# Graph attention and graph convolution in fp32: scores in seven half-size products over node halves of two graphs

## The chip, the cores and the metric

The kernel runs on one core of one Trainium2 chip. A core has TensorE (matrix multiplication, called PE in the profile), VectorE (DVE), ScalarE (ACT), GpSimd (POOL) and SyncE (SP, which here only issues transfers). Each engine works through its own instructions in order and waits for the others by semaphores. The metric is the time of one execution in microseconds of device time, and the figure compared is the median of several runs.

## What is computed

The input is 64 graphs of 256 nodes with 512 features each, and one 256 x 256 adjacency matrix per graph, all in fp32. Two layers follow each other, each with a residual:

```python
h = jnp.maximum(_layernorm(x, axis=-1), 0.0)
# layer 0: attention along the adjacency
query = jnp.einsum('bnd,od->bno', h, Wq_w) + Wq_b
keyt = jnp.einsum('bnd,od->bno', h, Wk_w) + Wk_b
value = jnp.einsum('bnd,od->bno', h, Wv_w) + Wv_b
weight = jnp.einsum('bqd,bkd->bqk', query, keyt)
weight = adj * jnp.exp(weight)
weight = weight / jnp.sum(weight, axis=2, keepdims=True)
x = x + jnp.einsum('bqk,bkd->bqd', weight, value)
# layer 1: graph convolution
h = jnp.maximum(_layernorm(x, axis=-1), 0.0)
A_hat = adj + jnp.eye(adj.shape[-1])
d_inv_sqrt = A_hat.sum(axis=-1) ** (-0.5)
L = A_hat * d_inv_sqrt[:, :, None] * d_inv_sqrt[:, None, :]
x = x + jnp.einsum('bij,bjf->bif', L, h @ W + b)
```

## The kernel before

The graphs are handled in 32 pairs (G = 2 graphs at a time, p is the number of the pair). A pair has 512 rows of x, held as four tiles of 128 rows (TB = 4), so that all projections work on 512 nodes at once. Query and key weights are multiplied into one matrix beforehand, so that the scores are h times a projected "key side" g.

Three of the large products of a pair are 512 x 512 x 512 each: the key side g (`key_side`), the values v (`values`) and the product of the aggregated features with the second layer's weight (`convolve`). Each is computed in `seven_products` (L321): a 2 x 2 block product with seven half-size products in place of eight, at the price of sums of blocks before and after. The sums of the features are t1 to t4 in the tile hS, made in `feature_sums` (L308) on GpSimd for every pair but the first. The feature matrix is stored transposed as hT, features over partitions and nodes along the free side. In it b11 and b21 are the columns of the first graph, b12 and b22 those of the second, with the first index for the half of the features. The sums of the weights are made once. The seven results land in three PSUM banks; a bank that holds one product is read by VectorE or ACT (first, u2, u3, c22) before a second product is added in the same bank, so that those two products depend on a quick reader.

The scores are not done in this way. `attend` (L464) handles one graph after the other. For each of two blocks of 128 keys it accumulates four matmuls with g as the stationary side and the graph's 256 query columns of hT as the moving one (L472). ACT takes the exponential out of PSUM into wT (L482), VectorE multiplies by the transposed adjacency aT (L483, both operands in SBUF), and then wT is the stationary side of the output matmuls (L493) against v. A column of ones in v gives the row sums. VectorE divides and adds into x (L503). After it GpSimd adds the identity to the diagonal blocks of aT (L741) and the value bias to x of the next pair (L683), and VectorE measures the rows for the second norm (L244).

`convolve` (L545) first aggregates: h times aT, four groups (`aggregate`, L551), each with two feature blocks and two blocks of nodes, and 256 columns moving (L555). The results and their sums are in yS, and the seven products with the second weight follow (pm_w). Their results are scaled by the degree and added into x by VectorE (`scaled`, L590) and GpSimd (`into`, L597). At the end of `second_layer` GpSimd makes the feature sums of the pair after next, and VectorE transposes its adjacency out of the tile aq, whose 32 x 32 blocks were placed by the transfers (`transposed_adjacency`, L452).

One step of the main loop for pair p is: `first_layer(p)` (attention), `project(p + 1)` (key side and values of the next pair, with norms and block transposes of pair p + 2 between), loads of x and adjacency for p + 3, and `second_layer(p)`. The order in which the instructions stand on each engine is set by a scheduler from these calls; `tc.issue_after` puts work behind a named instruction. The pools say how many buffers there are: xp has four for x, ap three for the adjacency, p1 one for each tag, p2 two, and PSUM eight banks. A load into a buffer waits for the last use of what was in it, and for x this is the transfer to the output. All these transfers are issued by SP, in one queue.

Of the kernel before, what the change touches and what calls it, by code (L numbers as in the profile page):

```python
# [16 lines left out]
def kernel(  # L17
# [29 lines left out]

    nc = tc.nc
# [16 lines left out]
    xp = ctx.enter_context(tc.tile_pool(name="xp", bufs=4))  # L65
    ap = ctx.enter_context(tc.tile_pool(name="ap", bufs=3))
# [7 lines left out]

    def load_x(p):
        x_tiles[p] = xp.tile([P, TB, D], F32, tag="x", name=f"x_{p}")
        nc.sync.dma_start(
            x_tiles[p], x[G * p : G * p + G].rearrange("g (nb p) d -> p (g nb) d", p=P)
        )

    def load_a(p):
        a_tiles[p] = ap.tile([P, TB, N], F32, tag="a", name=f"a_{p}")
        nc.sync.dma_start(
            a_tiles[p], adj[G * p : G * p + G].rearrange("g (nb p) k -> p (g nb) k", p=P)
        )
# [105 lines left out]
    def bias_products():  # L191
# [4 lines left out]
        g_rows, last = weighted_rows(wq_rows, bkT, "A2")  # L196
# [111 lines left out]
    def feature_sums(p, hT):  # L308
# [3 lines left out]
        hS = p1.tile([P, 4, 2, N], F32, tag="hS", name=f"hS_{p}")  # L312
        t1, t2, t3, t4 = (hS[:, i] for i in range(4))
# [3 lines left out]
        eng.tensor_tensor(t3, b22, b12, sub)  # L317
        eng.tensor_tensor(t4, b21, t2, sub)
        return (b11, b21, b22, t1, t2, t3, t4)
# [125 lines left out]
    def transposed_adjacency(p):  # L445
        a = a_tiles[p]
        aT = p2.tile([P, TB, N], F32, tag="aT", name=f"aT_{p}")
        if p > 0:
            out_view = aT.rearrange("p (g kt) q -> p kt g q", g=G)
            in_view = q_tiles[p].rearrange("p kt (g j) r -> p kt g (j r)", g=G)  # L450
            for kt in range(NB):
                nc.vector.transpose(out_view[:, kt], in_view[:, kt])  # L452
            return aT
        for g in range(G):
            pt = ps_m.tile([P, NB, N], F32, tag="pm", name=f"pt_a_{p}_{g}")
            for kb in range(NB):
                for qb in range(NB):
                    nc.tensor.transpose(  # L458
                        pt[:, kb, ts(qb, P)], a[:, g * NB + qb, ts(kb, P)], ident
                    )  # L460
            nc.scalar.copy(aT[:, g * NB : (g + 1) * NB, :], pt)
        return aT

    def attend(p, hT, gT, ks, aT):  # L464

        xt = x_tiles[p]
        wT = p1.tile([P, TB, N], F32, tag="wT", name=f"wT_{p}")
        for g in range(G):
            pm = ps_m.tile([P, NB, N], F32, tag="pm", name=f"pm_s_{p}_{g}")
            for kb in range(NB):  # L470
                for oc in range(DC):
                    nc.tensor.matmul(  # L472
                        pm[:, kb, :],
                        gT[:, oc, ts(g * NB + kb, P)],
                        hT[:, oc, ts(g, N)],
                        start=oc == 0,
                        stop=oc == DC - 1,
                    )
            rows = slice(g * NB, (g + 1) * NB)
            for kb in range(NB):  # L480
                t = g * NB + kb
                nc.scalar.activation(wT[:, t, :], pm[:, kb, :], AF.Exp, bias=ks[:, t : t + 1])  # L482
            nc.vector.tensor_tensor(wT[:, rows, :], wT[:, rows, :], aT[:, rows, :], mult)  # L483
        for g in range(G):
            for qb in range(NB):
                t = g * NB + qb
                rsum = sm.tile([P, 1], F32, tag="rsum", name=f"rsum_{p}_{t}")
                for half in range(2):
# [3 lines left out]
                    for kb in range(NB):  # L492
                        nc.tensor.matmul(  # L493
                            pm[:, 0:width],
                            wT[:, g * NB + kb, ts(qb, P)],
                            v[:, g * NB + kb, lo : lo + width],
# [6 lines left out]
                    last = nc.vector.scalar_tensor_tensor(xh, pm[:, 0:HD], rsum, xh, mult, add)  # L503
        return last.ins
# [13 lines left out]
    def weighted_degrees(p, d, row):  # L518
# [3 lines left out]
        scratch = p1.tile([P, D], F32, tag="scratch", name=f"ad_{p}")  # L522
        for t in range(TB):
            nc.vector.scalar_tensor_tensor(  # L524
                scratch[:, 0:N],
                a[:, t, :],
                1.0,
                row[:, ts(t // NB, N)],
# [16 lines left out]
    def convolve(p, h, aT, d, moved, then_t4, then_first):  # L545
# [5 lines left out]
        def aggregate(fh, g):  # L551
# [294 lines left out]
```

## Time and profile before

| what | value |
|---|---|
| median of 3 runs | 1861.83 us (1861.76 to 1861.85) |
| profiled execution | 1864.19 us, span of the profile 1862.4 us |
| PE busy | 1849.9 us (99%), 8578 matmul records and as many weight loads |
| DVE, ACT, POOL busy | 1235.8 us (66%), 760.8 us (41%), 641.8 us (34%) |
| matmuls by tile, records of 128x256 or 128x257 | pm_w 1792, pm_g 1792, pm_v 1792, pm_o 1024, pm_s 1024, pm_l 1024 |
| transfers | 114.83 MB, mean 62 GB/s; 1024 KB of x land 6.5 us after issue, the output 4.5 us |
| granted clock of TensorE | 0.998 |

One pair in mid-run takes 57.00 us. Its stages, by the engines' busy time in stretches of the profile (us from the start of the span; in each column the busy time and, in brackets, the number of instructions):

```profile
core 0: us, PE busy (x) PEld busy (x) DVE busy (x) ACT busy (x) POOL busy (x), PEclk, DMA share, GB/s
969.62:976.53 6.91, 6.91 (x34) 6.08 (x32) 2.78 (x5) 0.84 (x2) 4.79 (x6) 1.00 0.73 196
976.53:983.45 6.92, 6.92 (x33) 6.05 (x32) 5.71 (x16) 0.84 (x2) 5.08 (x6) 1.00 0.66 187
983.45:1007.63 24.18, 24.18 (x114) 21.27 (x113) 17.25 (x40) 13.17 (x21) 5.37 (x12) 1.00 0.03 8
1007.63:1014.53 6.90, 6.90 (x33) 6.08 (x32) 4.94 (x8) 1.17 (x2) 0.00 (x0) 1.00 0.04 14
1014.53:1026.62 12.09, 12.09 (x57) 10.64 (x56) 7.42 (x22) 7.80 (x14) 4.79 (x4) 1.00 0.13 44
```

The stretches are the scores, the outputs of the attention, the key side with the values, the aggregates, and the seven products with the second weight. A busy share of 100% on PE says that matmul records follow each other without a gap; PEld is the loading of the stationary side, which runs beside the matmuls. In the timeline a row is one group of like instructions: its start, its length from the first start to the last end, engine, line, operation, tiles and number, and in brackets the idle time of that engine before it with what ended it.

### The profile page before, as it was taken

To read this page: it belongs to the slowest core of one execution; us is meant where nothing else is said; L and a number is where in the kernel's file an instruction comes from. 1 tells how busy PE (TensorE), PEld (TensorE's weight loads), DVE (VectorE), ACT (ScalarE), POOL (GpSimd) and SP (SyncE) were. 2 spreads that over 40 slices of the span, in tenths; PEclk is the share of its full clock that TensorE was granted. 3 is DMA by queue.
4 is the path that set the end of the run, shared out by engine and by line. 5 is a ranking of instruction groups with operands and counts; after the bars stand their busy time and mean duration, and the time that the engine had idled before them with its cause. 6 is when DMAs were issued, how large, how long until landed. Compare 5 with 4: busy or idle time off the path is not lost.

```text
span 1862.4 us, 23484 instructions
## 1 busy us (share of the span) xinstructions
PE 1849.9 (99%) x8578; PEld 1625.5 (87%) x8578; DVE 1235.8 (66%) x2874; ACT 760.8 (41%) x1316; POOL 641.8 (34%) x839
## 2 busy tenths in 40 slices
PE   8999999999999999999999999999999999999998
PEld 7888888888888888888888888888888888888887
DVE  6866676666766666666667666666666676666745
ACT  3434443344434344443444344444434443344412
POOL 2443223432234432244322343322443223433222
PEclk9999999999999999999999999999999999999999
DMA  7322122221122231222221222202222112221001
GB/s 209 63 74 74 34 52 68 68 74 49 42 63 68 74 74 28 54 72 69 74 51 41 63 68 74 73 22 60 74 68 74 48 44 63 69 74 40 7 23 46
DMA packets 205908, 114.83 MB, mean 62 GB/s; under 512 B 148192, under 2 KB 168672, under 8 KB 205792
## 3 DMA queue, kind: packets, MB, share of 16 engines
q1 hardware_dynamic: 204672, 112.28, 23.0%
q8 instruction: 67, 1.10, 0.3%
q10 hardware_dynamic: 1056, 1.05, 0.2%
q14 instruction: 49, 0.40, 0.2%
q0 software_dynamic: 64, 0.00, 0.1%
HBM read 79.70 MB, written 33.62 MB: 61 GB/s over the span
## 4 chain that ended last, share of the span: by engine, by line
PE 98%; DVE 1%; DMA 1%; issue 0%; DVEq 0%; ACTq 0%
PE pm_g L338 21%; PE pm_w L338 21%; PE pm_v L338 21%; PE pm_o L493 12%; PE pm_l L555 12%; PE pm_s L472 11%; PE pm_mT L170 1%; DMA wq_rows<-in_L_gnn_Wq_w_dram 1%; DVE hc L275 0%; DVE ad L524 0%; PE pt_h L295 0%; PE pt_wv L220 0%; DVE aT L452 0%; DVE gT L389 0%; PE pt_a L458 0%
## 5 line engine op out<-in xcount | busy, mean ns | idle before, releaser
L338 PE MATMUL pm_w<-w_set,yS 128*128 128x256 f32 x1792 | 392.0, 379 | 0.0
L338 PEld LDWEIGHTS pm_w<-w_set,yS 128*128 128x128 f32 x1792 | 340.5, 190 | 46.3
L305 ACT COPY hT<-hq 32x512 f32<-32x512 f32 x496 | 305.5, 616 | 32.0 <-DVE hq L286 26.2
L597 POOL TENSOR_TENSOR x<-x,A_w 128x512 f32<-128x512 f32 x32 | 40.6, 1268 | 746.4 <-ACT A_w L588 746.4
L338 PE MATMUL pm_g<-hS,m_set 128*128 128x256 f32 x1024 | 236.5, 379 | 0.0
L338 PE MATMUL pm_v<-v_set,hS 128*128 128x256 f32 x1024 | 231.7, 379 | 1.5 <-DVE U_v L428 1.5
L493 PE MATMUL pm_o<-v,wT 128*128 128x257 f32 (+1 forms) x1024 | 226.8, 379 | 0.2 <-DVE wT L483 0.2
L472 PE MATMUL pm_s<-hT,gT 128*128 128x256 f32 x1024 | 226.4, 379 | 0.0
L555 PE MATMUL pm_l<-aT,h_b 128*128 128x256 f32 x1024 | 226.2, 379 | 0.0
L338 PEld LDWEIGHTS pm_v<-v_set,hS 128*128 128x128 f32 x1024 | 194.5, 190 | 28.3 <-DVE U_v L428 1.9
L493 PEld LDWEIGHTS pm_o<-v,wT 128*128 128x128 f32 x1024 | 193.7, 189 | 28.3 <-issue 0.5
L338 PEld LDWEIGHTS pm_g<-hS,m_set 128*128 128x128 f32 x1024 | 194.1, 190 | 27.1 <-DVE U_g L378 0.3
L555 PEld LDWEIGHTS pm_l<-aT,h_b 128*128 128x128 f32 x1024 | 194.6, 190 | 26.5
L472 PEld LDWEIGHTS pm_s<-hT,gT 128*128 128x128 f32 x1024 | 194.6, 190 | 26.5
L338 PE MATMUL pm_v<-v_set,hT 128*128 128x256 f32 x768 | 186.3, 379 | 0.0
L590 DVE SCALAR_TENSOR_TENSOR x<-pm_w,irr_d,x 128x256 f32<-128x256 f32 x256 | 112.1, 480 | 108.1 <-PE pm_w L338 82.6
L338 PE MATMUL pm_g<-hT,m_set 128*128 128x256 f32 x768 | 181.5, 379 | 0.0
L482 ACT ACTIVATE wT<-pm_s,ks 128x256 f32<-128x256 f32 x128 | 53.8, 471 | 290.8 <-PE pm_s L472 290.8
L338 PEld LDWEIGHTS pm_g<-hT,m_set 128*128 128x128 f32 x768 | 145.8, 190 | 20.4 <-issue 0.5
L338 PEld LDWEIGHTS pm_v<-v_set,hT 128*128 128x128 f32 x768 | 145.9, 190 | 19.8
L683 POOL TENSOR_TENSOR x<-x,bv_all 128x512 f32<-128x512 f32 x128 | 159.0, 1276 | 0.0
L483 DVE TENSOR_TENSOR wT<-wT,aT 128x512 f32<-128x512 f32 x64 | 44.3, 692 | 152.5 <-ACT wT L482 152.5
(119 smaller groups left out, 2085.6 us busy)
## 6 DMA issues: line engine op xcount, KB each, us to landing
x<-in_x_dram SPq DMA_DIRECT2D x32, 1024.0 KB, 6.5
out_dram<-x SPq DMA_DIRECT2D x31, 1024.0 KB, 4.5
a<-in_adj_dram SPq DMA_DIRECT2D x32, 512.0 KB, 3.9
aq<-in_adj_dram SPq DMA_DIRECT2D x124, 128.0 KB, 4.0
drow<-dflat SPq DMA_DIRECT2D x32, 256.0 KB, 5.0
wq_rows<-in_L_gnn_Wq_w_dram ACTq DMA_DIRECT2D x2, 512.0 KB, 8.4
wk_rows<-in_L_gnn_Wk_w_dram SPq DMA_DIRECT2D x2, 512.0 KB, 7.7
wv_rows<-in_L_gnn_Wv_w_dram SPq DMA_DIRECT2D x1, 1024.0 KB, 15.9
```

The source lines that it names most:

```text
L170: nc.tensor.matmul(pm, wk_rows[:, oc, ts(dc, P)], wq_rows[:, oc, ts(half, HD)], start=oc == 0, stop=oc == DC - 1,)
L305: last = nc.scalar.copy(dst[j * Q : (j + 1) * Q, i], src[i * Q : (i + 1) * Q, j])
L338: nc.tensor.matmul(banks[bank][:, r, :], left[:, ts(r, P)], right, start=start and r == 0 and dt == 0, stop=r == 1 and dt == 1, skip_group ...
L472: nc.tensor.matmul(pm[:, kb, :], gT[:, oc, ts(g * NB + kb, P)], hT[:, oc, ts(g, N)], start=oc == 0, stop=oc == DC - 1,)
L482: nc.scalar.activation(wT[:, t, :], pm[:, kb, :], AF.Exp, bias=ks[:, t : t + 1])
L483: nc.vector.tensor_tensor(wT[:, rows, :], wT[:, rows, :], aT[:, rows, :], mult)
L493: nc.tensor.matmul(pm[:, 0:width], wT[:, g * NB + kb, ts(qb, P)], v[:, g * NB + kb, lo : lo + width], start=kb == 0, stop=kb == NB - 1,)
L555: nc.tensor.matmul(pm[:, fi, :], h[:, g * NB + jb, ts(2 * fh + fi, P)], aT[:, g * NB + jb, :], start=jb == 0, stop=jb == NB - 1,)
L590: last = nc.vector.scalar_tensor_tensor(dst[:, r, :], pm[:, r, :], dr_, plus[:, r, :], mult, add)
L597: last = nc.gpsimd.tensor_tensor(block(i, g), block(i, g), more, add).ins
L683: nc.gpsimd.tensor_tensor(xh, xh, bv_all, add)
```

## The change

The scores become one seven-product scheme over the pair. For this the node halves are no longer the graphs: each graph's 256 nodes are split in two blocks of 128, and "half 0" is the first block of both graphs, "half 1" the second block of both. The tile order of x, adjacency, v and aT goes from graph-major to block-major (`p (nb g) k`). With this the sums t1 to t4 of the features serve the key side, the values and the scores. The score product is then, for each graph, keys in two blocks by queries in two blocks over two halves of the features: seven products, each of four matmuls (two graphs, two feature blocks) with 128 moving columns. The sums of the key side, s1 to s4, are made on GpSimd after each key side (`key_sums`); one of the four is written in place over a block of g, and likewise one feature sum over a block of hT. hS has two buffers instead of one, since the sums of a pair are now read until its attention.

The aggregates of `convolve` take a half of the nodes, so two graphs' blocks of 128 query columns in place of one graph's 256: twice as many matmuls, each with half the columns. The pools of x and of the adjacency lose one buffer each, and the loads for p + 3 move behind `second_layer(p)`. Each load of x and adjacency and each output transfer becomes two, one for each graph. The transposition of the adjacency for the pair after next moves from the end of the second layer to behind its u3 result, in four pieces of 256 columns instead of two of 512. One temporary (A2) goes; the second scaled copy is made in place.

The core of the diff:

```diff
-    xp = ctx.enter_context(tc.tile_pool(name="xp", bufs=4))
-    ap = ctx.enter_context(tc.tile_pool(name="ap", bufs=3))
+    xp = ctx.enter_context(tc.tile_pool(name="xp", bufs=3))
+    ap = ctx.enter_context(tc.tile_pool(name="ap", bufs=2))
...
+    def of_graph(tile_, g):
+        return tile_.rearrange("p (nb g) k -> p g nb k", g=G)[:, g]
+
+    def in_dram(t, p, g):
+        return t[G * p + g].rearrange("(nb p) k -> p nb k", p=P)
+
     def load_x(p):
         x_tiles[p] = xp.tile([P, TB, D], F32, tag="x", name=f"x_{p}")
-        nc.sync.dma_start(
-            x_tiles[p], x[G * p : G * p + G].rearrange("g (nb p) d -> p (g nb) d", p=P)
-        )
+        for g in range(G):
+            nc.sync.dma_start(of_graph(x_tiles[p], g), in_dram(x, p, g))
 
     def load_a(p):
         a_tiles[p] = ap.tile([P, TB, N], F32, tag="a", name=f"a_{p}")
-        nc.sync.dma_start(
-            a_tiles[p], adj[G * p : G * p + G].rearrange("g (nb p) k -> p (g nb) k", p=P)
-        )
+        for g in range(G):
+            nc.sync.dma_start(of_graph(a_tiles[p], g), in_dram(adj, p, g))
...
-        hS = p1.tile([P, 4, 2, N], F32, tag="hS", name=f"hS_{p}")
-        t1, t2, t3, t4 = (hS[:, i] for i in range(4))
+        hS = p2.tile([P, 3, 2, N], F32, tag="hS", name=f"hS_{p}")
+        t1, t2, t4 = (hS[:, i] for i in range(3))
         eng = nc.vector if p == 0 else nc.gpsimd
         eng.tensor_tensor(t1, b12, b11, sub)
         eng.tensor_tensor(t2, b22, t1, sub)
-        eng.tensor_tensor(t3, b22, b12, sub)
+
+        eng.tensor_tensor(b12, b22, b12, sub)
         eng.tensor_tensor(t4, b21, t2, sub)
-        return (b11, b21, b22, t1, t2, t3, t4)
+        return (b11, b21, b22, t1, t2, b12, t4)
+
+    def key_sums(p, gT):
+
+        a11, a21 = gT[:, 0:2, 0:N], gT[:, 0:2, N:NT]
+        a12, a22 = gT[:, 2:4, 0:N], gT[:, 2:4, N:NT]
+        gS = p1.tile([P, 3, 2, N], F32, tag="gS", name=f"gS_{p}")
+        s1, s2, s4 = (gS[:, i] for i in range(3))
+        nc.gpsimd.tensor_tensor(s1, a21, a22, add)
+        nc.gpsimd.tensor_tensor(s2, s1, a11, sub)
+
+        nc.gpsimd.tensor_tensor(a21, a11, a21, sub)
+        nc.gpsimd.tensor_tensor(s4, a12, s2, sub)
+        return (a11, a12, a22, s1, s2, a21, s4)
...
-        aT = p2.tile([P, TB, N], F32, tag="aT", name=f"aT_{p}")
+
+        aT = p2.tile([P, NB, NB, G, P], F32, tag="aT", name=f"aT_{p}")
         if p > 0:
-            out_view = aT.rearrange("p (g kt) q -> p kt g q", g=G)
             in_view = q_tiles[p].rearrange("p kt (g j) r -> p kt g (j r)", g=G)
             for kt in range(NB):
-                nc.vector.transpose(out_view[:, kt], in_view[:, kt])
+                for g in range(G):
+                    nc.vector.transpose(aT[:, kt, :, g, :], in_view[:, kt, g])
             return aT
...
-    def attend(p, hT, gT, ks, aT):
+    def attend(p, h_parts, g_parts, ks, aT):
 
         xt = x_tiles[p]
-        wT = p1.tile([P, TB, N], F32, tag="wT", name=f"wT_{p}")
-        for g in range(G):
-            pm = ps_m.tile([P, NB, N], F32, tag="pm", name=f"pm_s_{p}_{g}")
-            for kb in range(NB):
-                for oc in range(DC):
+        a11, a12, a22, s1, s2, s3, s4 = g_parts
+        b11, b21, b22, t1, t2, t3, t4 = h_parts
+
+        wT = p1.tile([P, NB, NB, G, P], F32, tag="wT", name=f"wT_{p}")
+        banks = {}
+
+        def product(bank, left, right, start=True):
+            if start:
+                banks[bank] = ps_m.tile([P, G, P], F32, tag="pm", name=f"pm_s_{p}_{bank}")
+            for g in range(G):
+                for dt in range(2):
                     nc.tensor.matmul(
-                        pm[:, kb, :],
-                        gT[:, oc, ts(g * NB + kb, P)],
-                        hT[:, oc, ts(g, N)],
-                        start=oc == 0,
-                        stop=oc == DC - 1,
+                        banks[bank][:, g, :],
+                        left[:, dt, ts(g, P)],
+                        right[:, dt, ts(g, P)],
+                        start=start and g == 0 and dt == 0,
+                        stop=g == 1 and dt == 1,
+                        skip_group_check=True,
                     )
-            rows = slice(g * NB, (g + 1) * NB)
-            for kb in range(NB):
-                t = g * NB + kb
-                nc.scalar.activation(wT[:, t, :], pm[:, kb, :], AF.Exp, bias=ks[:, t : t + 1])
-            nc.vector.tensor_tensor(wT[:, rows, :], wT[:, rows, :], aT[:, rows, :], mult)
-        for g in range(G):
-            for qb in range(NB):
-                t = g * NB + qb
+            return banks[bank]
+
+        def small(tag):
+            return p1.tile([P, G, P], F32, tag=tag, name=f"{tag}_{p}")
+
+        first, u2, u3, c22 = (small(tag) for tag in ("sA", "sU2", "sU3", "sC"))
+
+        def weights(kb, qb, scores):
+            block = wT[:, kb, qb]
+            for g in range(G):
+                t = kb * G + g
+                nc.scalar.activation(block[:, g], scores[:, g], AF.Exp, bias=ks[:, t : t + 1])
+            nc.vector.tensor_tensor(block, block, aT[:, kb, qb], mult)
+
+        pm0 = product(0, a11, b11)
+        nc.scalar.copy(first, pm0)
+        pm1 = product(1, s2, t2)
+        nc.vector.tensor_tensor(u2, pm1, first, add)
+        product(0, a12, b21, False)
+        weights(0, 0, pm0)
+        product(1, s3, t3, False)
+        nc.vector.tensor_tensor(u3, pm1, first, add)
+        pm2 = product(2, s1, t1)
+        nc.vector.tensor_tensor(c22, pm2, u3, add)
+        pm3 = product(3, a22, t4)
+        nc.vector.tensor_tensor(u3, pm3, u3, add)
+        weights(1, 0, u3)
+        weights(1, 1, c22)
+        product(2, s4, b22, False)
+        nc.vector.tensor_tensor(u2, pm2, u2, add)
+        weights(0, 1, u2)
...
-        def aggregate(fh, g):
-            pm = ps_m.tile([P, 2, N], F32, tag="pm", name=f"pm_l_{p}_{g}_{fh}")
+        def aggregate(fh, qb):
+            pm = ps_m.tile([P, 2, N], F32, tag="pm", name=f"pm_l_{p}_{qb}_{fh}")
             for fi in range(2):
-                for jb in range(NB):
-                    nc.tensor.matmul(
-                        pm[:, fi, :],
-                        h[:, g * NB + jb, ts(2 * fh + fi, P)],
-                        aT[:, g * NB + jb, :],
-                        start=jb == 0,
-                        stop=jb == NB - 1,
-                    )
+                for g in range(G):
+                    for jb in range(NB):
+                        nc.tensor.matmul(
+                            pm[:, fi, ts(g, P)],
+                            h[:, jb * G + g, ts(2 * fh + fi, P)],
+                            aT[:, jb, qb, g, :],
+                            start=jb == 0,
+                            stop=jb == NB - 1,
+                        )
...
-            last = scaled(a2, a, 0)
-            into(1, 0, None, a2)
+            last = scaled(a, a, 0)
+            into(1, 0, None, a)
...
+        def u3(pm):
+            with tc.issue_after(scaled(s3, pm, 1, a1)):
+                then_u3()
...
+        key_parts[p] = key_sums(p, keys[p])
...
-        attend(p, hTs[p], keys[p], terms[p], aTs[p])
+        attend(p, parts[p], key_parts[p], terms[p], aTs[p])
...
+        def then_u3():
+            if nxt < NP:
+                aTs[nxt] = transposed_adjacency(nxt)
...
             with tc.issue_after(ends["pool"]):
                 parts[nxt] = feature_sums(nxt, hTs[nxt])
-            with tc.issue_after(ends["vector"]):
-                aTs[nxt] = transposed_adjacency(nxt)
...
-        if p + 3 < NP:
-            load_x(p + 3)
-            load_a(p + 3)
         if p == NP - 1:
             second_layer(p - 1, NP)
         if p != NP - 2:
             second_layer(p, p + 2)
+        if p + 3 < NP:
+            load_x(p + 3)
+            load_a(p + 3)
```

## The prediction

> **What bounds the kernel now.** I read the page first: the busy shares (part 1) and the chain that ended last (part 4).
>
> ```profile
> span 1862.4 us, 23484 instructions
> PE 98%; DVE 1%; DMA 1%; issue 0%; DVEq 0%; ACTq 0%
> ```
>
> TensorE is the chain almost everywhere, so only two things can change the time: the sum of matmul passes, and waits put in front of them. Next the groups by shape:
>
> ```profile
> L472 PE MATMUL pm_s<-hT,gT 128*128 128x256 f32 x1024 | 226.4, 379 | 0.0
> L555 PE MATMUL pm_l<-aT,h_b 128*128 128x256 f32 x1024 | 226.2, 379 | 0.0
> ```
>
> Each fp32 matmul of the code is two records ("passes"), each with its own weight load: 16 matmuls x 32 pairs x 2 = 1024. Then the timeline of one pair in mid-run. Call the start of its scores X = 969.62:
>
> ```profile
> 964.64 0.88 DVE L590 SCALAR_TENSOR_TENSOR U_w<-pm_w,irr_d,A_w 128x256 f32<-128x256 f32 x2 [0.85 <-PE pm_w L338]
> 966.37 0.88 DVE L590 SCALAR_TENSOR_TENSOR x<-pm_w,irr_d,x 128x256 f32<-128x256 f32 x2 [0.85 <-PE pm_w L338]
> 967.33 1.27 POOL L597 TENSOR_TENSOR x<-x,U_w 128x512 f32<-128x512 f32 x1 [2.96 <-DVE x L590]
> 968.55 1.26 POOL L315 TENSOR_TENSOR hS<-hT 128x512 f32<-128x512 f32 x1
> 969.62 7.07 PE L472 MATMUL pm_s<-hT,gT 128*128 128x256 f32 x32
> 972.36 1.27 POOL L318 TENSOR_TENSOR hS<-hT,hS 128x512 f32<-128x512 f32 x1
> 973.28 0.84 ACT L482 ACTIVATE wT<-pm_s,ks 128x256 f32<-128x256 f32 x2 [6.46 <-PE pm_s L472]
> 974.15 0.69 DVE L483 TENSOR_TENSOR wT<-wT,aT 128x512 f32<-128x512 f32 x1 [2.17 <-ACT wT L482]
> 976.53 7.09 PE L493 MATMUL pm_o<-v,wT 128*128 128x257 f32 x32
> ...
> 1026.62 3.62 PE L472 MATMUL pm_s<-hT,gT 128*128 128x256 f32 x16
> ```
>
> The period is 1026.62 - 969.62 = 57.00 us for 264 passes: 215.9 ns each, without a gap. The reader should also see that GpSimd's last feature sum ends at 973.63, just before the adjacency product at 974.15. Last, the start-up, the only place with 128-column passes at full clock:
>
> ```profile
> 25.87 1.95 PE L295 MATMUL pt_h<-ident,h_a 128*128 128x128 f32 x16
> 27.65 1.91 PE L220 MATMUL pt_wv<-ident,wv_rows 128*128 128x128 f32 x16
> 29.40 1.04 PE L458 MATMUL pt_a<-ident,a 128*128 128x128 f32 x8
> ...
> 24.62 1.08 PEld L203 LDWEIGHTS pc_gb<-ones_sq,wr_A 128*128 128x128 f32 x8
> 25.62 0.30 PEld L206 LDWEIGHTS pc_gb<-bs,ones_sq 128*128 128x128 f32 x2
> ```
>
> (29.40 - 27.65)/16 = 109.4 ns for a transpose pass. In the bias products the moving side is one column, so weight loads alone set the pace: 1.00 us less the first, which still waits out a 216 ns pass, over 7 is 112 ns.
>
> **What the Trainium skill says.** "TensorE: Matmul & The Clock Gate", section "Back-to-back issue gap", states that in a stream of loads and matmuls both set the spacing, 81 ns at 128 columns where the matmul alone would take about 56; the transposes here show no such surplus, but they are another mode. Its section "LDWEIGHTS (loading the stationary operand)" gives columns/1.2, 107 ns for 128; the trace has 112. "GPSIMD Engine Reference", section "Key points", says GpSimd shares its SBUF interfaces with VectorE and contends with instructions that have two SBUF inputs. The trace agrees, in the start-up (ad reads a and drow, both in SBUF):
>
> ```profile
> 61.67 1.33 POOL L318 TENSOR_TENSOR hS<-hT,hS 128x512 f32<-128x512 f32 x1
> ...
> 61.02 0.85 DVE L524 SCALAR_TENSOR_TENSOR ad<-a,drow 128x256 f32<-128x256 f32 x1
> 61.91 1.37 DVE L524 SCALAR_TENSOR_TENSOR ad<-a,drow 128x256 f32<-128x256 f32 x1
> ```
>
> Alone this takes 0.42; begun under a GpSimd sum it ends 0.28 us after that sum does (63.00, then 63.28). In steady state no such VectorE instruction overlaps a GpSimd sum.
>
> **The change, part by part.** From the program's own order, which shows 28 half-size score matmuls:
>
> 1. Passes. Scores 32 x 256 columns become 56 x 128; aggregates L555, whose query blocks of one graph no longer lie together, go from 32 x 256 to 64 x 128. With T for a 128-column pass: 64 x 215.9 = 13.82 us become 120 T. T lies between 109.4 and 112 by the two rows; I take 110.5, so 13.26, a gain of 0.56 per pair if nothing waits. Break-even is T = 115.1.
>
> 2. The wait I expect. Times after X: product k ends at 8(k+1)T, and its result can be read 0.20 later (in the trace exps start at 973.28 = 0.20 after 16 passes). P2 ends 2.65, exps of block (0,0) (two of 128 columns, by L482's 0.42 pitch less 128 columns at about 0.83 ns) end 3.54, and its adjacency product wants VectorE at 3.57. It has two SBUF inputs. Where is GpSimd? The transposes of the next adjacency (L452) move ahead of the c22 result. Four of 256 at about 0.34 pitch (half of L286's 0.62 with its fixed part) start at X - 4.18 (U_w's end at -4.10, less the 0.08 by which neighbours on VectorE overlap), so c22 starts at -2.82 instead of -3.25 and ends at -1.94; GpSimd's x+U3 starts 0.08 later as now, and then the sums in the new order t1, t2, t3, t4 with the trace's steps 1.22, 1.36 (dependent), 1.23, 1.23: t4 runs from 3.18 to 4.45. So the (0,0) product is caught under t4 and ends at 4.45 + 0.28 = 4.73. Behind it on VectorE stand the u3 add (0.42) and the c22 add (0.42; 256-column adds are the 0.69 of 512 less 256 columns), ending at 5.07 and 5.53. The last score product accumulates into the bank that c22 reads: 0.05 for the semaphore and 0.10 for restarting the weight pipeline (the start-up's only U_v stall shows both), so it starts at 5.69, not at 48T = 5.30. The stage lasts 5.69 + 8T = 6.57 against 6.91: -0.34. Of the fully hidden gain of 0.72 here, about half goes.
>
> 3. The chain behind it: u3' add, exps and product (1,0) end near 7.50; the output matmuls have three first halves of block (0,0) to run (6 x 0.216), so they want it at 7.87 less 0.15. Hidden, by 0.2; bound 0 to 0.4 if another GpSimd diagonal add (0.45) gets in first. I take 0.
>
> 4. Aggregates: 64T = 7.07 against 6.90: +0.17. Moved transposes: the last pm_w product needs c22's bank by -1.73 - 0.15, c22 ends -1.94 + 0.05: +0.03, bounds 0 and 0.25.
>
> 5. Key sums: four GpSimd adds, 1.27 each, 163 us in all, run from about 997.1 to 1002.2 in this pair's clock, under U_v and hq (one SBUF tensor input each); hc, which has two, starts at 1003.25: hidden with 1 us to spare. They are wanted at the next X, 24 us later. In the prologue they follow four bias adds and do meet hc, which was already stretched to 1.24 and 1.63 us there: +1.5 once, bounds 0 and 2.5.
>
> 6. Buffers. x(p+3) now waits for out(p): out at X + 1.2, 4.5 to land, about 1 to issue x, 6.5 to land: X + 13.2. Its bn_stats come at 987.79 = X + 18.2. Hidden by some 4 us. Adjacency, with two buffers, waits for the weighted degrees, where it is issued now (960.81). Split transfers add SP issues of about 0.4 us each in a queue that mostly waits. The smaller VectorE and ACT pieces (some +3 and +1.3 us a pair) lie where those engines wait for PE (VectorE 38.1 busy of 57.0).
>
> Sum: -0.34 + 0.17 + 0.03 = -0.14 for 31 pairs; the last, with no feature sums beside it, -0.72 + 0.17 = -0.55; +1.5: -3.4 us. The profiled execution took 1864.19 (span 1862.4 and 1.8 around it), 2.4 above the runs' median 1861.83; the difference carries over: 1864.19 - 3.4 = 1860.8 there, **1858.4** for the median. With T at 109.4 or 112 this case gives 1856 or 1862.
>
> **Rivals.**
> - *Hidden after all.* If t4 starts 0.4 us later than worked out, the (0,0) product is caught under t3 only and nobody waits: -0.55 x 32 + 1.5 = -16 us, **1846** (1842 with T = 109.4). For it: every other deadline holds, by 0.1 us. Against: the feature sums fill GpSimd over the whole critical stretch.
> - *Slower: a 128-column pass costs more than the transposes show.* With the stall, the change turns into a loss from T = 112.5 on. If a third of the skill's surplus of 25 ns appears, T is about 118: scores 5.69 + 0.94 = -0.28, aggregates 7.55 = +0.65, so +0.40 x 32 + 1.5: **1876**. For it: real fp32 loads measure 112 already, and the new streams are 56 and 64 passes long with waits between. Against: the transposes' 109.4.
> - *Late x.* Should the loads land 2 us after they are wanted beyond the slack, VectorE stands before U_g with PE behind it, up to 1 us a pair after: **1887**. Against: 4 us of slack.
>
> **How the numbers follow.** Chances: the forecast 0.58, hidden 0.14, dearer passes 0.20, late x 0.08. 0.2% is 3.7 us, about what this kernel's runs can tell from no change. The forecast is near that bound: of its 0.58, 0.27 is faster, 0.25 same, 0.06 slower (own range 1851 to 1866). Hidden is faster; of the dearer passes 0.02 is same, the rest slower with late x. Faster 0.41, same 0.27, slower 0.32. The range 1842 to 1878 leaves out late x and the worse passes.
>
> **What would show it.** Right: a period near 56.9; a gap of about 0.4 us before the last four score matmuls, with the (0,0) product stretched to some 1.2 us and ending 0.28 after GpSimd's fourth sum; aggregates of 7.0 to 7.1. Wrong: aggregates above 7.2 (T), no stretched product (hidden), or bn_stats of the fresh x waiting for DMA.

## The result, and the profile after

The changed kernel takes 1866.84 us (1865.99 to 1868.54, ten runs) beside 1862.14 for the kernel before in the same session: a ratio of 1.0026, 95% interval 1.0017 to 1.0036. It is slower by 4.7 us where 3.4 us less was forecast. The profiled execution took 1865.99 us and is the quickest of the ten, so what its trace adds up to need not match the medians to the last microsecond.

The page of the changed kernel, its span, busy shares (time, share, instructions) and the chain of waits:

```profile
span 1864.2 us, 28019 instructions
...
PE 1846.3 (99%) x10370; PEld 1668.7 (90%) x10370; DVE 1346.6 (72%) x3160; ACT 802.2 (43%) x1476; POOL 818.8 (44%) x967
...
PE 94%; DVE 3%; POOL 1%; ACT 1%; issue 1%; DVEq 0%; POOLq 0%
```

TensorE's own share of the chain falls from 98% to 94%: VectorE and GpSimd now set the end in places. The same pair in mid-run as in the table of stages before, with the same columns (stretch and length, then the busy time of each engine with its instructions):

```profile
972.56:979.18 6.62, 6.51 (x58) 6.35 (x56) 3.94 (x8) 2.08 (x7) 5.15 (x6) 1.00 0.64 189
979.18:986.10 6.92, 6.92 (x34) 6.06 (x33) 6.33 (x19) 0.89 (x3) 6.21 (x6) 1.00 0.57 168
986.10:1010.28 24.18, 24.18 (x113) 21.27 (x112) 17.69 (x40) 13.17 (x21) 9.67 (x15) 1.00 0.09 12
1010.28:1017.43 7.15, 7.15 (x66) 7.15 (x65) 5.00 (x8) 1.17 (x2) 0.00 (x0) 1.00 0.00 0
1017.43:1029.52 12.09, 12.09 (x59) 10.64 (x58) 8.56 (x26) 7.80 (x14) 4.44 (x4) 1.00 0.25 62
```

The scores take 6.62 us instead of 6.91 and contain the only hole in PE (6.51 busy). The aggregates take 7.15 instead of 6.90, and there the second busy figure, that of the weight loads, fills the stretch. The other three stages are as before. The period is 1029.52 - 972.56 = 56.96 us against 57.00: the gain in the scores and the loss in the aggregates all but cancel.

The timeline of that pair's scores shows the hole. Group rows give start, length, engine and line:

```profile
975.65 1.27 POOL L326 TENSOR_TENSOR hS<-hT,hS 128x512 f32<-128x512 f32 x1
...
976.10 1.10 DVE L520 TENSOR_TENSOR wT<-wT,aT 128x256 f32<-128x256 f32 x1 [1.06 <-ACT wT L519]
...
977.04 1.06 PE L500 MATMUL pm_s<-hS,gT 128*128 128x128 f32 x8
977.12 0.41 DVE L529 TENSOR_TENSOR sU<-pm_s,sA 128x256 f32<-128x256 f32 x1
...
977.64 0.42 DVE L531 TENSOR_TENSOR sC<-pm_s,sU 128x256 f32<-128x256 f32 x1
...
978.18 0.97 PEld L500 LDWEIGHTS pm_s<-hT,gS 128*128 128x128 f32 x8 [0.27 <-POOL aT L801]
978.21 1.13 PE L500 MATMUL pm_s<-hT,gS 128*128 128x128 f32 x8
```

The adjacency product (L520) starts under GpSimd's fourth feature sum, which ends at 976.92, and ends at 977.20, 0.28 later. The u3 add (L529) and the c22 add (L531) stand behind it, and the last score product, which adds into c22's bank, starts at 978.21 instead of 977.93, where the pass before it would have let it. The profile puts this wait down to a diagonal add on GpSimd (aT, L801), but that add is not what is waited for: in all 32 pairs of this trace the load of this product starts 0.12 us after the c22 add has ended, also in the first and the last pair, where the diagonal adds ahead of it had ended some 0.9 us before.

The pair's last adjacency product (L520, from 980.56) is held too, under the first of the value-bias adds on GpSimd: it takes 1.39 us in place of 0.41. No matmul waits for it.

So mid-run gives next to nothing and costs nothing; the loss lies at the start. From the first key-side product to the first output product of the second pair the kernel before takes 90.45 us, the changed one 97.13. The page's groups do not show this, the timeline of the first pair does:

```profile
45.63 1.25 DVE L282 SCALAR_TENSOR_TENSOR hc<-h_a,c_all 128x512 f32<-128x512 f32 x1
...
46.92 1.64 DVE L282 SCALAR_TENSOR_TENSOR hc<-h_a,c_all 128x512 f32<-128x512 f32 x1
...
47.97 1.72 POOL L335 TENSOR_TENSOR gS<-gT 128x512 f32<-128x512 f32 x1
...
48.60 1.64 DVE L282 SCALAR_TENSOR_TENSOR hc<-h_a,c_all 128x512 f32<-128x512 f32 x1
...
49.76 1.60 POOL L336 TENSOR_TENSOR gS<-gS,gT 128x512 f32<-128x512 f32 x1
...
50.28 1.63 DVE L282 SCALAR_TENSOR_TENSOR hc<-h_a,c_all 128x512 f32<-128x512 f32 x1
...
51.84 0.68 DVE L449 TENSOR_TENSOR U_v<-pm_v,A_v 128x512 f32<-128x512 f32 x1
...
52.58 3.68 PE L359 MATMUL pm_v<-v_set,hS 128*128 128x256 f32 x8 [3.38 <-DVE U_v L449]
...
56.09 1.89 PE L359 MATMUL pm_v<-v_set,hT 128*128 128x256 f32 x8
```

All four scalings of the second pair's features (hc) are held, first by the bias adds and then by the key sums (L335, L336), U_v stands behind them, and TensorE waits 3.38 us for it. In the kernel before only the first two of the four are held, by the bias adds (POOL, L683), the others take 0.69 us each (one is shown), and the wait for U_v is 1.50 us:

```profile
46.04 5.41 POOL L683 TENSOR_TENSOR x<-x,bv_all 128x512 f32<-128x512 f32 x4
...
49.09 1.24 DVE L275 SCALAR_TENSOR_TENSOR hc<-h_a,c_all 128x512 f32<-128x512 f32 x1
...
50.37 1.63 DVE L275 SCALAR_TENSOR_TENSOR hc<-h_a,c_all 128x512 f32<-128x512 f32 x1
...
52.05 0.69 DVE L275 SCALAR_TENSOR_TENSOR hc<-h_a,c_all 128x512 f32<-128x512 f32 x1
...
54.14 1.99 PE L338 MATMUL pm_v<-v_set,hS 128*128 128x256 f32 x8 [1.50 <-DVE U_v L428]
```

A second loss stands in the matmul row of the changed kernel: its eight passes take 3.68 us, not 1.99. They start 427 ns apart, twice 216: TensorE's clock was halved. The Trainium skill, "TensorE: Matmul & The Clock Gate", Part 1, section "What's actually happening", says that the clock falls to half after an idle window of about 3.4 us, and that this window runs freely. The trace agrees here: the profile grants half the clock from 52.65 to 56.06 us, and in the stretch of the same 3.41 us before it TensorE was busy for 0.07 us. How idle such a window has to be is taken up in the last section.

The step of pair 1 has a wait of its own. There the sums of the second layer's weights (L156 to L159), made once, meet the key sums of that pair:

```profile
86.17 1.77 DVE L158 TENSOR_TENSOR w_set<-w_set,w 128x512 f32<-128x512 f32 x1
...
87.47 1.60 POOL L336 TENSOR_TENSOR gS<-gS,gT 128x512 f32<-128x512 f32 x1
...
91.21 0.68 DVE L441 TENSOR_TENSOR U_v<-pm_v,A_v 128x512 f32<-128x512 f32 x1
...
91.94 1.99 PE L359 MATMUL pm_v<-v_set,hT 128*128 128x256 f32 x8 [2.46 <-DVE U_v L441]
```

The pass gaps add up: 1.8 more of waiting for U_v of pair 0 (3.66 from pass to pass in place of 1.88), 1.7 of halved clock, 2.7 for U_v of pair 1, and a remainder of 0.5, most of it in pair 0's scores and outputs: 6.7 us. The 29 periods that follow give 1.1 back. From the first output product of pair 30 to the end the kernel before takes 1862.4 - 1774.5 = 87.9 us, the changed one 1864.2 - 1776.6 = 87.6: another 0.3 less. Together this is 6.7 - 1.1 - 0.3 = +5.3 after the first key-side product; the medians differ by 4.7. What lies before that product waits for the first weights and differs between executions of one and the same part of the program (it starts at 31.13 in the profile of before, 27.66 in that of the changed kernel, 29.10 in that of fewer_buffers below), so the last 0.6 us are not assigned.

### The profile page after: what moved, and what is told of

Its sections match the earlier page's. It is cut to its first block, busy times and chain, and to the rows that moved or that the text cites. A ratio compares the mean times of both kernels' runs of the same rounds, so it can differ in the third digit from the quotient of the medians.

```text
span 1864.2 us, 28019 instructions
## 1 busy us (share of the span) xinstructions
PE 1846.3 (99%) x10370; PEld 1668.7 (90%) x10370; DVE 1346.6 (72%) x3160; ACT 802.2 (43%) x1476; POOL 818.8 (44%) x967
## 4 chain that ended last, share of the span: by engine, by line
PE 94%; DVE 3%; POOL 1%; ACT 1%; issue 1%; DVEq 0%; POOLq 0%
PE pm_g L359 21%; PE pm_w L359 21%; PE pm_v L359 20%; PE pm_l L611 12%; PE pm_o L548 12%; PE pm_s L500 7%; DVE wT L520 2%; POOL aT L801 1%; ACT wT L519 1%; PE pm_mT L177 1%; DVE hc L282 0%; PE pm_run_in L169 0%; DVE ad L579 0%; PE pt_h L302 0%; DVE w_set L157 0%
## 5 line engine op out<-in xcount | busy, mean ns | idle before, releaser
L359 PE MATMUL pm_v<-v_set,hT 128*128 128x256 f32 x1024 | 242.0, 379 | 2.5 <-DVE U_v L441 2.5
L359 PE MATMUL pm_g<-hT,m_set 128*128 128x256 f32 x1024 | 236.7, 379 | 0.0
L611 PE MATMUL pm_l<-aT,h_b 128*128 128x128 f32 x2048 | 233.8, 275 | 0.0
L359 PEld LDWEIGHTS pm_v<-v_set,hT 128*128 128x128 f32 x1024 | 194.6, 190 | 29.4 <-DVE U_v L441 2.9
L359 PEld LDWEIGHTS pm_g<-hT,m_set 128*128 128x128 f32 x1024 | 194.5, 190 | 27.0 <-issue 0.5
L359 PE MATMUL pm_v<-v_set,hS 128*128 128x256 f32 x768 | 178.3, 382 | 3.4 <-DVE U_v L449 3.4
L359 PE MATMUL pm_g<-hS,m_set 128*128 128x256 f32 x768 | 181.3, 379 | 0.0
L520 DVE TENSOR_TENSOR wT<-wT,aT 128x256 f32<-128x256 f32 x128 | 104.5, 816 | 52.8 <-ACT wT L519 52.8
L653 POOL TENSOR_TENSOR x<-x,U_w 128x512 f32<-128x512 f32 x64 | 81.3, 1270 | 105.6 <-DVE x L646 105.6
L268 ACT ACTIVATE h_b<-x,nb_b,rs_b 128x512 f32<-128x512 f32 x128 | 93.8, 803 | 62.6 <-POOL nb_b L261 62.6
```

What stands on the lines that cost most here:

```text
L268: nc.scalar.activation(h[:, t, :], x_tiles[p][:, t, :], AF.Relu, bias=nb[:, t : t + 1], scale=rd[:, t : t + 1],)
L359: nc.tensor.matmul(banks[bank][:, r, :], left[:, ts(r, P)], right, start=start and r == 0 and dt == 0, stop=r == 1 and dt == 1, skip_group ...
L520: nc.vector.tensor_tensor(block, block, aT[:, kb, qb], mult)
L611: nc.tensor.matmul(pm[:, fi, ts(g, P)], h[:, jb * G + g, ts(2 * fh + fi, P)], aT[:, jb, qb, g, :], start=jb == 0, stop=jb == NB - 1,)
L653: last = nc.gpsimd.tensor_tensor(block(i, g), block(i, g), more, add).ins
```

## The experiments

Beside these kernels the kernel before took 1861.7 to 1862.1 us.

**agg_halves.** The kernel before, with only the aggregates cut in two. It prices a 128-column pass.

```diff
-                for jb in range(NB):
+                for qb in range(NB):
+                    for jb in range(NB):
...
-                        pm[:, fi, :],
+                            pm[:, fi, ts(qb, P)],
...
-                        aT[:, g * NB + jb, :],
+                            aT[:, g * NB + jb, ts(qb, P)],
```

> The kernel before, with each aggregate matmul of 256 moving columns cut in two of 128; nothing else is changed and the result is the same. Theory A (a 128-column pass is bound by its weight load, 111.6 ns as in the trace of after): the aggregates of a pair go from 6.91 to 64 x 0.1116 = 7.14 us, the period from 57.00 to 57.24, the total by +7.5 us to about 1869.6. Rival (the pace of the transposes, 109.4 ns, is the real one, and the rest in the trace of after comes from its waits): 7.00 us, period 57.09, total about 1865.

1869.44 us (1869.28 to 1869.48), ratio 1.0040 [1.0026, 1.0054]. Its timeline:

```profile
1009.07 7.31 PE L556 MATMUL pm_l<-aT,h_b 128*128 128x128 f32 x64
1016.21 12.25 PE L338 MATMUL pm_w<-w_set,yS 128*128 128x256 f32 x56
```

64 passes in 1016.21 - 1009.07 = 7.14 us, 111.6 ns each, and a period of 57.24, as theory A had it. A real fp32 pass of 128 columns follows the one before at the spacing of the start-up's weight loads (112), not at the 109.4 of the transposes. That the weight load sets this pace is read from the loads, which lie back to back in the aggregates of the changed kernel (7.15 of 7.15 us); it was not tested by itself. Over 32 pairs the cut comes to 7.7 us; 7.4 were measured.

**fewer_buffers.** The kernel before, with one buffer less for x and adjacency and the loads behind `second_layer`.

```diff
-    xp = ctx.enter_context(tc.tile_pool(name="xp", bufs=4))
-    ap = ctx.enter_context(tc.tile_pool(name="ap", bufs=3))
+    xp = ctx.enter_context(tc.tile_pool(name="xp", bufs=3))
+    ap = ctx.enter_context(tc.tile_pool(name="ap", bufs=2))
```

> The kernel before with three buffers for x and two for the adjacency, and the loads for p + 3 placed behind the second layer; the result is the same. Theory A: nothing, 1861.5 to 1862.7, period 57.00. Rival D (late loads are part of the loss): VectorE waits for a transfer before bn_stats of the fresh pair, and 1 to 5 us of the 4.7 us loss appear here.

1861.95 us, ratio 0.9999 [0.9991, 1.0008], and a period of 57.00: the buffers cost nothing.

**keys_idle.** fewer_buffers, with four key sums after each key side whose results nothing reads.

```diff
+        nc.gpsimd.tensor_tensor(s1, a21, a22, add)
+        nc.gpsimd.tensor_tensor(s2, s1, a11, sub)
+        nc.gpsimd.tensor_tensor(s3, a11, a21, sub)
+        nc.gpsimd.tensor_tensor(s4, a12, s2, sub)
...
         keys[p], last = key_side(p, parts[p], then_g, ahead(measure, p + 1), nothing)
+        key_sums(p, keys[p])
```

> The kernel before with the buffers and the place of the loads of after, and with four GpSimd sums over the key side of each pair into a tile of their own that nobody reads; the output stays the reference's. Theory A (key sums cost only where VectorE has instructions with two SBUF inputs beside them: hc of pair 1 in the prologue, the sums of the second layer's weight in pair 1): period stays 57.00 from pair 2 on, TensorE waits 3 to 5 us longer up to the second pair's outputs, total 1865 to 1869. Rival C (key sums slow VectorE in every pair): the period rises by 0.1 us or more, with no new gap in the prologue.

1868.43 us (1866.18 to 1871.42), ratio 1.0035 [1.0023, 1.0048]. The period stays at 57.00, and the stretch from the first key-side product to the second pair's outputs is 96.25 instead of 90.45 us. Its timeline of the first pair has the stall of the changed kernel, with the score matmuls of before:

```profile
50.53 1.63 DVE L275 SCALAR_TENSOR_TENSOR hc<-h_a,c_all 128x512 f32<-128x512 f32 x1
...
51.58 1.71 POOL L330 TENSOR_TENSOR gS<-gT 128x512 f32<-128x512 f32 x1
...
54.51 3.59 PE L350 MATMUL pm_v<-v_set,hS 128*128 128x256 f32 x8 [3.38 <-DVE U_v L440]
```

Even the halved clock is there (eight passes in 3.59). Key sums that nobody waits for therefore cost 5.8 us at the start (6.4 by the medians) and nothing afterwards: contention with VectorE, not lateness of their results. Theory A holds, with a wait somewhat longer than its 3 to 5 us, and rival C falls with the period.

**product_later.** The changed kernel, with the first adjacency product behind the c22 add on VectorE. `weights` is parted into its exps and its product for this.

```diff
-        weights(0, 0, pm0)
+        exps(0, 0, pm0)
...
-        nc.vector.tensor_tensor(c22, pm2, u3, add)
+        with tc.issue_after(nc.vector.tensor_tensor(c22, pm2, u3, add).ins):
+            by_adjacency(0, 0)
```

> The changed kernel with one move: on VectorE the adjacency product of block (0,0) is issued behind the c22 add instead of in front of the u3 add; the result is the same. Theory A (the held product delays u3 and c22, and c22 delays the last four score matmuls): no product stretched to 1.1 us in the score stage, the gap of 0.27 us before the last score product gone, period 56.6 to 56.7 and a total of 1855 to 1858; if a diagonal add on GpSimd now catches the (1,0) product, up to 0.3 us of it comes back in front of the outputs (up to 1866). Rival E (the gap is the plain chain of adds, whatever GpSimd does): gap and period (56.96) stay.

1857.44 us (1856.80 to 1858.47), ratio 0.9976 [0.9966, 0.9986]; 9.4 us less than the changed kernel, and faster than the kernel before. The timeline:

```profile
971.75 1.27 POOL L326 TENSOR_TENSOR hS<-hT,hS 128x512 f32<-128x512 f32 x1
...
972.44 0.42 DVE L536 TENSOR_TENSOR sU<-pm_s,sA 128x256 f32<-128x256 f32 x1 [1.31 <-PE pm_s L500]
...
973.33 0.42 DVE L538 TENSOR_TENSOR sC<-pm_s,sU 128x256 f32<-128x256 f32 x1 [0.47 <-PE pm_s L500]
973.67 0.41 DVE L523 TENSOR_TENSOR wT<-wT,aT 128x256 f32<-128x256 f32 x1
...
974.02 1.06 PE L500 MATMUL pm_s<-hT,gS 128*128 128x128 f32 x8
```

The adds, each with one operand in PSUM, pass under GpSimd's sum at full speed; the product comes after it and takes 0.41 instead of 1.10. The last score product starts 0.89 after the one before it (973.13), eight passes of 111.6: no hole. The scores take 6.28 us, and the period is 56.61: theory A, and rival E falls.

**weight_sums_later.** The changed kernel, with the once-only weight sums behind the values of pair 1 rather than in front.

```diff
-        if p == 1:
-            with tc.issue_after(last):
-                weight_sums(w1_set, w1_21)
...
         with tc.issue_after(last.ins):
+            if p == 1:
+                weight_sums(w1_set, w1_21)
             add_graph_bias(p - 1)
```

> The changed kernel with one edit in the start-up: the sums of the second layer's weights, made once in the step of pair 1 on VectorE (two SBUF inputs each), stand behind that pair's values instead of in front of them. Theory A (they run against the key sums on GpSimd, and U_v of pair 1 is late by their stretch): the 2.5 us of waiting in front of the last value products of pair 1 goes, 1866.8 - 2.5 = 1864.3 (1863.5 to 1865.0). Theory B (U_v is late for another reason, such as the block transposes ahead of it): the wait stays, 1866 to 1868.

1863.58 us (1862.74 to 1864.01), 3.3 less than the changed kernel, as theory A had it. The wait of pair 1 is gone. In its profile the clock was not halved in pair 0 either, though the pass gap there was 3.64 us against 3.66: with a window that runs freely, a matter of where the gap falls. Here it is shared out over two windows, in each of which TensorE was busy for 1.7 of 3.41 us. Another wait there grew (a score gap of 1.97 instead of 0.77). By the trace 2.7 comes from the weight sums; that the clock's 1.7 less that gap's 1.2 makes up the rest is the arithmetic of one profile.

**norm_terms_later.** In addition, hc of pair 1 behind the values of pair 0.

```diff
-            then_u2=lambda: find_terms(1),
+            then_u2=nothing,
...
             weigh_degrees(0)
+            find_terms(1)
```

> The edit of weight_sums_later, and in addition the scaling of pair 1's features (hc, four VectorE instructions with two SBUF inputs) issued behind the values of pair 0 instead of inside them. Theory A (hc under the key sums holds up U_v of pair 0, TensorE waits 3.4 us, and its clock is halved for the passes after it, about 2 us more): both go, 1864.3 - 5.3 = 1859.0 (1857.5 to 1861). Theory B (pair 1's features are then late, and the wait comes back in front of its key side): 1863 or more.

1863.47 us (1861.79 to 1865.50): nothing further, so theory A falls. In the profile, which is the quickest of thirteen executions and lies 1.7 us under their median, the wait for U_v is gone and the clock stays up, but a new wait of nearly the same size stands in the scores of pair 0, not in front of pair 1's key side as theory B had it. What the slower executions lose is not shown. The timeline:

```profile
56.74 1.44 POOL L325 TENSOR_TENSOR hT<-hT 128x512 f32<-128x512 f32 x1
...
58.15 1.78 POOL L326 TENSOR_TENSOR hS<-hT,hS 128x512 f32<-128x512 f32 x1
...
58.74 1.21 DVE L590 TENSOR_TENSOR ds<-s,irr_d 128x4 f32<-128x4 f32 x1
59.87 0.41 DVE L525 TENSOR_TENSOR sU<-pm_s,sA 128x256 f32<-128x256 f32 x1
...
60.42 1.13 PE L500 MATMUL pm_s<-hT,gT 128*128 128x128 f32 x8 [3.01 <-DVE sU L525]
```

The u2 add (L525), which TensorE waits for, is queued behind the weighted degrees of pair 0 (L579 to L590), whose instructions have two SBUF inputs and now meet the feature sums of pair 1. Even `ds`, four columns that take 0.14 in the changed kernel, lasts until GpSimd's sum is over.

**both_fixes.** norm_terms_later with product_later, and the diagonal adds held until the last adjacency product.

```diff
+            with tc.issue_after(last_product):
+                last = nc.gpsimd.tensor_tensor(diag, diag, ident, add)
```

> The edits of norm_terms_later, with the first adjacency product behind the c22 add as in product_later, and the GpSimd diagonal adds held back until the last adjacency product is done. Theory A (the losses are independent): 1857.4 - (1866.8 - 1859.0) = 1849.6 (1848 to 1852), a period of 56.6 us. Theory B (what was late behind the start-up waits shows up elsewhere): 1854 to 1857.

1855.25 us (1854.85 to 1856.54), ratio 0.9966 [0.9952, 0.9979], period 56.61. The time is that of theory B, and of adding what the two edits had really given (1857.44 - 3.4 = 1854.1) with 1.2 left over. In the profile TensorE's clock is halved for 6.83 us (from 60.94 on) in pair 0's scores and outputs.

**wide_aggregates.** both_fixes with aggregates of 256 columns: one group holds, for one feature block, both query blocks of both graphs. Evacuations become twice as many, of half the size.

```diff
-                            pm[:, fi, ts(g, P)],
+                        pm[:, :, g, :],
...
-                            aT[:, jb, qb, g, :],
+                        aT[:, jb, :, g, :],
```

> both_fixes with the aggregates back at 256 moving columns: one group holds both query blocks of both graphs for one feature block, so the moving side is two runs of 128 columns. Theory A (a pass of 256 columns takes 215.9 ns also when they lie in two runs, 64 passes in 6.91 us instead of 7.15): 0.24 x 32 = 7.7 us less than both_fixes, 1842 (1840 to 1844.5), a period of 56.4 us. Theory B (the evacuations, now of 256 columns and more in number, come late for the seven products, or a moving side in two runs is slower): 1848 or more.

1847.67 us (1847.47 to 1848.68), ratio 0.9925 [0.9913, 0.9937]: 7.6 less than both_fixes, where 7.7 was reckoned. The absolute value expected is missed because it was reckoned from the 1849.6 that both_fixes should have taken, and not from its 1855.25. The timeline:

```profile
1001.01 7.07 PE L620 MATMUL pm_l<-aT,h_b 128*128 128x256 f32 x32
1007.91 12.25 PE L359 MATMUL pm_w<-w_set,yS 128*128 128x256 f32 x56
```

6.90 us for 32 passes (the expectation's 64 is the number of the halved ones), 215.9 ns each as in the kernel before, and a period of 56.37: the halved columns were not a price of the new block order.

**quiet_start.** wide_aggregates, with the weighted degrees of pair 0 and hc of pair 1 behind pair 0's last adjacency product.

```diff
-        with tc.issue_after(last.ins):
-            weigh_degrees(0)
-            find_terms(1)
...
+        if p == 0:
+            with tc.issue_after(last_product):
+                weigh_degrees(0)
+                find_terms(1)
```

> wide_aggregates, with the weighted degrees of pair 0 and the scaling of pair 1's features (hc) both issued behind the last adjacency product of pair 0, since neither is wanted before. Theory A (in norm_terms_later, both_fixes and wide_aggregates the wait moved into the scores of pair 0 only because these VectorE instructions stand ahead of its u2 add and are held by GpSimd's sums): the stalls of 3.1 us before and 1.8 us after the second group of score products there go, and perhaps the halved clock with them: 1847.7 - 4.9 = 1842.8 (1840.5 to 1844.5). Theory B (the work is then late where it lands, in front of the key side of pair 1): 1846 or more.

1841.91 us (1841.91 to 1842.19), ratio 0.9893 [0.9877, 0.9910]: 5.8 less than wide_aggregates, and 20 us less than the kernel before. The timeline of pair 0's scores:

```profile
54.42 0.42 DVE L532 TENSOR_TENSOR sU<-pm_s,sA 128x256 f32<-128x256 f32 x1
...
54.44 2.05 PE L500 MATMUL pm_s<-hT,gT 128*128 128x128 f32 x16 [0.23 <-ACT sA L530]
```

The u2 add is no longer queued behind anything, and 0.23 us of waiting is left. Theory A holds, with a part of theory B: a gap of 2.2 us at 71.9 now stands in the key side of pair 1. Much of the gain is the clock: in the profile of wide_aggregates it is halved for 10.24 us from 59.68 on, in which TensorE is busy for 7.7, and in this profile it is not halved in this stretch. Half of that busy time, 3.9 us, is an estimate of what the clock had cost there.

## Why the prediction was wrong

| term | forecast | measured |
|---|---|---|
| scores, a pair | -0.34 | -0.29 |
| aggregates, a pair | +0.17 | +0.25 |
| moved transposes, a pair | +0.03 | no loss seen |
| period | -0.14 | -0.04 |
| first key-side product to the second pair's outputs | +1.0 | +6.7 |
| the 29 periods after it | -4.1 | -1.1 |
| from pair 30's outputs to the end | -0.4 | -0.3 |
| sum | -3.4 | +5.3 |

The last four rows lay the forecast's sum over the stretches that were measured. The first of them holds the start-up's +1.5 and also two score stages and the aggregates of one pair (-0.5); the third holds the last pair's scores and two pairs' aggregates.

**Step 5, the key sums, is where it failed.** "In the prologue they follow four bias adds and do meet hc [...]: +1.5 once, bounds 0 and 2.5" stands against a stretch that lost 5.7 us more than forecast. The collision that it names was there and had about the right price: TensorE's wait for U_v of pair 0 grew by 1.8. Two other costs were put at nothing without a reason. The longer wait left TensorE idle for nearly all of a 3.41 us window, and its clock was halved for the next (1.7). And the weight sums of pair 1, two SBUF inputs each, stand in the same stretch of VectorE as that pair's key sums (2.7): the step looked at a steady pair and at the first, not at work that is done once in the second. keys_idle shows nearly all of it without the rest of the change, and weight_sums_later takes the 2.7 away. For a steady pair the step was right: the last key sum ends at 1004.94, and hc starts at 1005.91.

**Step 1, T, was too low.** 110.5 was chosen between 109.4 and 112; it is 111.6 (agg_halves). Of the two rows that of the weight loads came nearer. By the forecast's own sum this makes -0.06 of -0.14 a pair, some 2.3 of the 3.0 us that the 29 periods fell short. The rival of dearer passes had the right sign of this and the wrong size: T = 118 does not occur, nor do the skill's 81 ns at 128 columns ("TensorE: Matmul & The Clock Gate", "Back-to-back issue gap") for fp32 here. Its break-even, 112.5, is about that of the period alone; the forecast's whole sum, with the +1.5 of the start-up, turns into a loss from 112.0 on, as its own 1862 us for T = 112 says. Neither was reached.

**Step 2 was right**, down to the instruction: the product caught under the fourth sum, ending 0.28 after it, u3 and c22 behind it, scores of 6.62 against 6.57 forecast. product_later shows it from the other side, by taking the wait away.

**Step 3** held: the outputs follow the scores at once. **Step 4**'s aggregates are step 1 again. **Step 6** held, though its own sum leaves 5.0 us of slack where it says some 4: fewer_buffers costs nothing, and the rival of late x falls with it. The rival "hidden after all" did not occur, but most of its gain was real: the same product behind the adds brings the period to 56.61, -0.39 where -0.55 was reckoned with the lower T.

By the traces the error is 8.7 us: 5.7 from the start-up, 3.0 from the periods, next to nothing from the end. By the medians it is 8.1, and the 0.6 between them lie before the first key-side product. With the start-up as forecast, the result would have been 0.4 (by the traces) to 1.0 us (by the medians) under the kernel before, within what can be told from no change; the sign was decided there. Of the signs that were to show the forecast right, the period, the gap (0.28 us instead of 0.4) and the stretched product came true, and the aggregates (7.15) missed narrowly: all of them look at a steady pair, and none at the place where the time was lost.

## What to carry to other kernels

Work put on GpSimd is priced by what VectorE does beside it: look for VectorE instructions with two SBUF inputs in every stretch it can fall into, the first steps and once-only work among them, and for who is queued behind them. Where one such instruction cannot be avoided, let those that TensorE waits for, and that read PSUM, go ahead of it. Halving the columns of a matmul from 256 to 128 cost 3.4% a column here (two passes of 111.6 ns for one of 215.9); ask whether a moving side in two runs keeps them whole. After a wait of some microseconds on TensorE, look at the granted clock of the passes behind it too.

## What was not expected of the hardware

- Under a GpSimd sum a VectorE instruction with two SBUF inputs reads like one that waits for the sum's end and then runs through its columns: it ends 0.55 us after it with 512 columns (hc, at 50.24 and 51.91 in the changed kernel, the sums at 49.69 and 51.36), 0.28 with 256, and 0.02 with four (`ds` in norm_terms_later, at 59.95, the sum at 59.93). The GpSimd side is held too: a sum of 1.27 takes up to 1.78.
- fp32 passes of 128 columns follow each other at 111.6 ns with their weight loads back to back; transposes at 109.4. A moving side of two runs of 128 columns costs no more than one of 256.
- It is not the length of a wait that decides whether TensorE's clock is halved. In every trace of this case the granted clock keeps its value for whole multiples of 3.41 us, and which clock a window of that length has goes with how long TensorE was busy in the window before it:

| kernel | gap between passes, us | window, us | TensorE busy in it, us | clock after it |
|---|---|---|---|---|
| the changed kernel | 3.66 | 49.24 to 52.65 | 0.07 | half |
| product_later | 3.64 | 50.73 to 54.15 | 0.80 | half |
| wide_aggregates | 3.29 | 56.27 to 59.68 | 1.37 | half |
| norm_terms_later | 3.29 | 55.79 to 59.20 | 1.62 | full |
| weight_sums_later | 3.64 | 51.03 to 54.45 | 1.73 | full |

A window in which TensorE works for 0.80 or 1.37 us is not the idle window that the Trainium skill names in the section cited above, and yet half the clock follows; here the measurement decides. In the eleven traces of this case the border lies between 1.37 and 1.53 us of 3.41. The clock came back after windows that were busy for 3.26 us or more, and not after those busy for 2.26 or less. Why the border lies there is not shown.
